# A fused graph-network kernel: messages by a seven-product scheme, sums of h made two blocks ahead, and earlier loads in the front

## The chip, the cores and the metric

The kernel runs on one core of a Trainium2 chip. The metric is device time in microseconds (us) for one execution of the whole program. The profile shows the five engines: PE (TensorE), with its weight loads apart as PEld, DVE (VectorE), ACT (ScalarE), POOL (GpSimd) and SP (SyncE, which here only issues DMAs). ACT also issues DMAs, from its own instruction stream.

## What is computed

Two layers on `x` of shape 128 x 128 x 256 (128 graphs of 128 nodes), all in fp32:

```python
# layer 0, with h = relu(layernorm(x))
s   = h @ w_se.T + b_se                                   # 3 columns
A   = exp(-(sq_i + sq_j - 2 s_i.s_j)) * adj                # sq = sum(s * s)
msg = relu(h @ w_msg.T + b_msg)                            # 256 columns
x_nmp  = A @ msg
x_conv = relu(bn2(conv1d_17(relu(bn1(conv1d_1(h))))) + h)
gi = [x_conv, x_nmp] @ w_ih.T + b_ih;  gh = h @ w_hh.T + b_hh
x  = x + GRU(gi, gh, h)                                    # r, z, n gates
# layer 1: on the first 25 nodes of each graph, five groups of two graph convolutions
```

The rows that the change is about are `msg` and `s`. They are one matrix product, with the 3 columns of `w_se` set beside the 256 of `w_msg`.

## The kernel before

The 128 graphs are worked through in 32 blocks of 4 graphs (`BB`, `NBLK`). h is held transposed: a tile `ht` of 128 partitions (half of the 256 features) x 2 halves x 512 columns (4 graphs x 128 nodes). A bank is one of eight PSUM tiles of 512 fp32 columns, and they are handed out in turn (`bank()`, L92).

**Front.** The 17-wide convolution is done in the frequency domain, for two halves of 64 graphs each. First `weight_spectra` (L158) turns the taps of the convolution into spectra, eight times: taps come in by `taps_load` (L152) into `w2`, four groups of 32 traced matmuls (L165) follow, ACT and DVE copy the banks out (L173, L171), and ACT writes the result to memory (`vd`, L175). Between these groups `heads` (L264) works block by block on the first 64 graphs: `head_load` (L180) brings x in, `head_stats` and `head_norm` do the layer norm on DVE and POOL, `head_turn` transposes it to `ht` (L212) and writes it to memory (`htd`, L214), `head_conv1` (L226) and `head_spectra` (L241) follow. Then `spectral` (L285) multiplies the spectra: for every pair of frequencies it loads a tile `v` from `vd` (L294, three buffers), sums it on POOL (L309), and runs L312 and L317. The second half of the graphs goes through `heads` and `spectral` again. Its first three blocks are begun by `heads_begin` (L251), whose loads are issued from ACT. In the second `spectral`, POOL also makes the weight sums of the gates, a few at a time (`gate_weights`, L331).

In the part of the front up to the end of the first `heads`, the order is written out by hand. So are SP's up to the end of the second `heads`, and POOL's up to the end of the front. Everything else is put in order by a scheduler, which decides each engine's order when the program is built; each engine then works through its own order strictly.

**Gate blocks.** From then on, 32 blocks follow. `gates` (L592) computes three gates by a seven-product scheme: the 256 x 512 product is cut into 2 x 2 quarters, and seven products of quarters, with sums of weights (`sw`) and sums of data (`t`) as operands, take the place of eight. A `unit` (L602) is such a set of seven: each product j has a bank of its own, and is taken out by ACT (`m1`, `m5`: L615, L623), DVE (L617, L620, L627, L630, L633) or POOL (`u4`, L625, which adds two tiles in SBUF; L631). The sums of data come from `gate_inputs` (L578): for xc (the conv branch) and h on POOL, for xn (the message branch) on DVE, four additions each (L586 to L589). They are made in `nxt` (L1021), which runs as a hook at the product j == 4 of the last unit.

After every product, `step` (L1006) lets other work in, alternately one step of `beside_gates` (L954) for the next block and one step of layer 1. `beside_gates(i + 1)` does that block's `messages` (L509), `conv_out` (L490), `edge_terms` (L532), `edges` (L541) and `x_nmp` (L556). In `messages`, each of the 4 graphs has two matmuls of 259 columns with h as the stationary operand (L516), and DVE adds the bias, once for the message (L517) and once for s (L518); ACT does the Relu (L520). The matmuls of `x_nmp` (L563) are 128 columns wide, those of the conv output (L498) too. Between the front and the gate blocks, DVE makes the degrees of layer 1's graphs (`degrees`, L694, with the reduction L698 that waits for a load).

SP's order of loads for a gate block is `load` (L446): ht, adjacency, and the inverse transform's inputs ym and yr.

Of the kernel before, what the change touches and what calls it, by code (L numbers as in the profile page):

```python
# [8 lines left out]
F32 = mybir.dt.float32  # L9
# [4 lines left out]
P = 128  # L14
# [12 lines left out]
HID = 512  # L27

# [46 lines left out]
def gnn_kernel(ctx: ExitStack, tc: tile.TileContext, io, out0: bass.AP, out1: bass.AP):  # L75
# [38 lines left out]
    def constant_loads():  # L114
        nc.sync.dma_start(vec, io["vec"])
        nc.sync.dma_start(wc1, io["wc1"].rearrange("(c p) o -> p c o", p=P))
        nc.sync.dma_start(fd, io["fd"])
# [34 lines left out]
    def taps_load(pool, c, q, queue, split=1):  # L152
        w2 = pool.tile([P, WCH // 4, P], F32, tag="w2", name="w2", bufs=2)
        for t in range(0, WCH // 4, WCH // 4 // split):
            queue.dma_start(w2[:, t:t + WCH // 4 // split], io["w2t"][:, c, q, t:t + WCH // 4 // split])
        return w2
# [94 lines left out]
    def heads_begin(wk, xk, ahead, h):  # L251

        i = h * NBH
        for k in range(ahead):
            head_load(xk, ahead, i + k, nc.scalar)
        yield
        for k in range(3):
            head_stats(wk, i + k)
            yield
            if k < 2:  # L260
                head_norm(i + k)
        head_turn(wk, i)
# [68 lines left out]
    def gate_weights():  # L331
        tt = nc.gpsimd.tensor_tensor
        for k in range(3):
            a11, a12, a21, a22 = gate_blocks(k)
            s2, s3, s4 = (sw[k][:, :, j] for j in range(3))
            tt(s3, a11, a21, op=ALU.subtract)
            tt(a21, a21, a22, op=ALU.add)
            yield
            tt(s2, a21, a11, op=ALU.subtract)
            tt(s4, a12, s2, op=ALU.subtract)  # L340
            yield

    with front as es:
# [7 lines left out]
        with ExitStack() as ws:  # L351
# [8 lines left out]
            taps = [taps_load(wp, *todo[0], nc.sync, split=4)]  # L360
            head_load(xk, ahead, 0, nc.scalar)
            spectra = []

            def some_spectra(k=1):
                for _ in range(k):
                    if not spectra and todo:
                        spectra.append(weight_spectra(wp, *todo.pop(0), taps.pop(0)))
                    if spectra and next(spectra[0], STOP) is STOP:
                        spectra.pop(0)
                        if len(todo) > 1:  # L370
                            taps.append(taps_load(wp, *todo[1], nc.scalar))
                        some_spectra()
# [6 lines left out]
            nc.sync.dma_start(fw, row("fw", 5))  # L379
            head_stats(hk, 0)  # L380
            some_spectra()
            head_norm(0)
            some_spectra()
            head_turn(hk, 0)
            consts = constants()
            next(consts)
            some_spectra()
            head_stats(hk, 1)
# [12 lines left out]
        wms = gw.tile([P, C, D + 3], F32)  # L401
        bms = gw.tile([P, D + 3], F32)
# [4 lines left out]
        def small_loads():  # L407
            nc.sync.dma_start(idm, io["idm"])
            nc.sync.dma_start(wms, io["wms"].rearrange("(c p) o -> p c o", p=P))
            nc.sync.dma_start(bms, row("bms", D + 3))  # L410
# [79 lines left out]
    def conv_out(i):  # L490
# [4 lines left out]
        for o in range(C):  # L495
# [7 lines left out]
            u = wk.tile([P, T], F32, tag="el", name="u", bufs=2)  # L503
            nc.vector.scalar_tensor_tensor(u, ps, sc2[:, o:o + 1], ht[:, o, :], op0=ALU.mult, op1=ALU.add)  # L504
            nc.scalar.activation(xc[:, o, :], u, AF.Relu, bias=sh2[:, o:o + 1])
# [3 lines left out]
    def messages(i):  # L509

        ht = hts[i]
        msg = wk.tile([P, BB, D], F32, tag="msg", name="msg", bufs=1)
        for b in range(BB):
            ps = bank()
            for c in range(C):
                nc.tensor.matmul(ps[:, :D + 3], ht[:, c, b * N:(b + 1) * N], wms[:, c, :], start=c == 0, stop=c == C - 1)  # L516
            nc.vector.tensor_tensor(msg[:, b, :], ps[:, :D], bms[:, :D], op=ALU.add)  # L517
            nc.vector.tensor_tensor(lr[:, 1, b, 0:3], ps[:, D:D + 3], bms[:, D:], op=ALU.add)  # L518
            if b % 2:
                nc.scalar.activation(msg[:, b - 1:b + 1, :], msg[:, b - 1:b + 1, :], AF.Relu)  # L520
                if b == 1:
                    yield
        msgs[i] = msg
        sv = lr[:, 1, :, 0:3]
        nc.vector.tensor_scalar(lr[:, 0, :, 0:3], sv, 2.0, None, op0=ALU.mult)
        s2 = wk.tile([P, BB, 3], F32, tag="sse", name="sse", bufs=2)
        nc.vector.tensor_mul(s2, sv, sv)
        nc.vector.reduce_sum(lr[:, 1, :, 3:4], s2, axis=AX.X)
        nc.vector.tensor_scalar(lr[:, 0, :, 4:5], lr[:, 1, :, 3:4], -1.0, None, op0=ALU.mult)
        yield  # L530
# [25 lines left out]
    def x_nmp(i):  # L556
# [3 lines left out]
        for c in range(C):  # L560
# [4 lines left out]
            if c:  # L565
# [12 lines left out]
    def gate_inputs(i, which=(0, 1, 2)):  # L578

        tt = ts.setdefault(i, {})  # L580
        for k in which:
            d, eng = ((xcs, nc.gpsimd), (xns, nc.vector), (hts, nc.gpsimd))[k]
            d = d[i]
            t = wk.tile([P, 4, H], F32, tag=f"t{k}", name=f"t{k}")
# [401 lines left out]
    degs = degrees(*degree_loads())  # L986
    begin = beside_gates(0)
    while 0 not in A_s:
        next(begin)
    gate_inputs(0, (2, 0))  # L990
# [11 lines left out]
    for i in range(NBLK):  # L1002
# [18 lines left out]
        def nxt():  # L1021
            for _ in first:
                pass
            if i + 1 < NBLK:
                gate_inputs(i + 1)
# [58 lines left out]
def _lay_out(a):  # L1084
# [21 lines left out]
    d["wms"] = cc(np.concatenate([w["w_msg"], w["w_se"]]).T)  # L1106
    d["bms"] = cc(np.concatenate([w["b_msg"], w["b_se"]]))
# [60 lines left out]
```

## Time and profile before

| | |
|---|---|
| runs | 1913.9, 1918.53, 1918.58 us; median 1918.53 |
| the profiled execution's own time | 1919.48 us |
| its span | 1917.7 us |
| mean granted TensorE clock | 0.995 |
| front, up to the first gate block's matmuls | about 490 us |
| one gate block without layer 1 beside it | 36.92 us |
| L516, messages' matmuls | x512, 128x259, 385 ns mean of one |
| L563, x_nmp's matmuls | x512, 128x128, 275 ns mean of one |
| L517 on DVE | x128, 414 ns mean of one |
| L625 on POOL | x128, 728 ns mean of one |

A line such as `L612 PE MATMUL bank<-t,sw 128*128 128x256 f32 x1152 | 291.6, 380` reads: line 612 of the kernel, on TensorE, writes a bank from the tiles t and sw, 1152 instructions with 128 x 256 elements, 291.6 us busy in all, 380 ns each. Matmuls are pipelined, so the duration of one is longer than the distance from one to the next: L516 has 385 ns, while eight of them in a row take 1.75 us. The distance is what counts for TensorE's time. "idle before, releaser" at the end of a line says how long the engine had stood idle and what ended it. The chain of work is followed back from the last instruction; each piece is a start, a duration and what ran. ACTq and SPq are DMA issues from ACT and SP.

### The profile page before, as it was taken

The page shows a single profiled execution, that of the slowest core. Times are in us where ns is not written, and L with a number is a line of the kernel's source. Part 1 is how long each engine was busy: PE and PEld are TensorE (multiplying, and loading weights), DVE is VectorE, ACT ScalarE, POOL GpSimd, SP SyncE. Part 2 cuts the span into 40 slices and gives each one's busy share as a digit, 9 for nine tenths or more (in the row PEclk, how much of TensorE's full clock was granted, in tenths as well). Part 3 has the DMA queues.
Part 4 walks back from the last instruction along what each step waited for, and adds up shares of the span by engine and source line. Part 5 has one row for each costly group of instructions (what it writes and reads, how often), then busy time and mean ns, then how long its engine had stood idle before and what let it go on. Part 6 is the DMA issues. An engine that isn't in the chain of part 4 may idle for free.

```text
span 1917.7 us, 30432 instructions
## 1 busy us (share of the span) xinstructions
PE 1890.3 (99%) x10610; PEld 1646.4 (86%) x10610; DVE 1303.9 (68%) x3247; ACT 720.5 (38%) x1555; POOL 609.1 (32%) x678
## 2 busy tenths in 40 slices
PE   8999999999999999999999999999999999999998
PEld 7888889988788888888888888888888888888887
DVE  5676557744677777777666677777756677787643
ACT  4553114411333343343343443333343434334334
POOL 1012531255234334433322233433322233443300
PEclk9999999999999999999999999999999999999999
DMA  8786896379842333333234433233334434222135
GB/s 322 288 312 226 297 311 235 121 241 306 256 117 73 74 95 76 81 90 106 71 94 97 130 97 87 73 82 108 75 90 97 144 72 107 65 78 71 36 92 151
DMA packets 248872, 265.81 MB, mean 139 GB/s; under 512 B 106866, under 2 KB 223943, under 8 KB 244239
## 3 DMA queue, kind: packets, MB, share of 16 engines
q1 hardware_dynamic: 236639, 196.70, 36.9%
q10 hardware_dynamic: 12080, 67.16, 9.0%
q8 instruction: 85, 1.39, 0.3%
q14 instruction: 68, 0.56, 0.1%
HBM read 178.66 MB, written 85.14 MB: 138 GB/s over the span
## 4 chain that ended last, share of the span: by engine, by line
PE 88%; DMA 4%; DVE 4%; issue 2%; ACT 1%; POOL 1%; SPq 0%; ACTq 0%; POOLq 0%; DVEq 0%
PE bank L612 45%; PE bank L317 6%; PE bank L516 5%; PE bank L937 5%; PE bank L877 5%; PE bank L226 4%; PE bank L312 3%; PE bank L563 3%; PE bank L498 3%; PE bank L241 3%; PE bank L165 2%; PE bank L501 1%; PE bank L788 1%; PE bank L856 1%; DMA v<-vd 1%
## 5 line engine op out<-in xcount | busy, mean ns | idle before, releaser
L612 PE MATMUL bank<-t,sw 128*128 128x256 f32 x1152 | 291.6, 380 | 0.7 <-DVE u L504 0.7
L625 POOL TENSOR_TENSOR u<-u,m 128x256 f32<-128x256 f32 x128 | 93.2, 728 | 612.7 <-ACT m L623 545.0
L612 PEld LDWEIGHTS bank<-t,sw 128*128 128x128 f32 x1152 | 215.8, 191 | 31.1 <-issue 2.3
L612 PE MATMUL bank<-t,wih 128*128 128x256 f32 x768 | 197.2, 379 | 0.0
L612 PEld LDWEIGHTS bank<-t,wih 128*128 128x128 f32 x768 | 143.4, 190 | 19.3 <-issue 0.5
L309 POOL TENSOR_TENSOR vs<-v 128x512 f32<-128x512 f32 x78 | 101.3, 1318 | 114.8 <-DMA v<-vd 49.4
L516 PE MATMUL bank<-wms,ht 128*128 128x259 f32 x512 | 124.1, 385 | 0.0
L226 PE MATMUL bank<-wc,ht 128*128 128x256 f32 x512 | 121.4, 391 | 1.6 <-ACT ht L213 1.6
L612 PE MATMUL bank<-xn,wih 128*128 128x256 f32 x384 | 114.9, 381 | 3.6 <-DVE xn L566 3.6
L612 PE MATMUL bank<-t,whh 128*128 128x256 f32 x384 | 115.0, 381 | 0.0
L612 PE MATMUL bank<-xc,wih 128*128 128x256 f32 x384 | 114.8, 381 | 0.0
L937 PE MATMUL bank<-w,hh 128*125 128x256 f32 (+9 forms) x480 | 113.5, 380 | 1.0 <-DVE hh L882 1.0
L226 PEld LDWEIGHTS bank<-wc,ht 128*128 128x128 f32 x512 | 98.0, 196 | 16.7 <-ACT ht L213 3.5
L516 PEld LDWEIGHTS bank<-wms,ht 128*128 128x128 f32 x512 | 98.3, 192 | 15.1
L612 PE MATMUL bank<-ht,whh 128*128 128x256 f32 x384 | 109.9, 380 | 0.0
L877 PE MATMUL bank<-ax,w 128*128 128x500 f32 (+8 forms) x416 | 107.0, 396 | 0.7 <-DMA w<-in_w_dram 0.7
L520 ACT ACTIVATE msg<-msg 128x512 f32<-128x512 f32 x64 | 40.3, 630 | 174.1 <-DVE msg L517 174.1
L630 DVE TENSOR_TENSOR u<-bank,u 128x256 f32<-128x256 f32 x128 | 53.7, 420 | 73.6 <-PE bank L612 73.5
L196 POOL TENSOR_TENSOR rs<-ve,mhalf 128x4 f32<-128x4 f32 x32 | 32.3, 1009 | 217.8 <-DVE ve L194 217.8
L307 DVE SCALAR_TENSOR_TENSOR s<-X 128x256 f32<-128x256 f32 x78 | 47.3, 612 | 79.4 <-PE bank L317 79.1
L937 PEld LDWEIGHTS bank<-w,hh 128*125 128x125 f32 (+9 forms) x480 | 84.3, 177 | 19.2 <-DVE hh L882 1.4
L657 ACT ACTIVATE nn<-nn,vec 128x512 f32<-128x512 f32 x64 | 46.2, 722 | 133.4 <-DVE nn L656 133.4
(187 smaller groups left out, 4279.5 us busy)
## 6 DMA issues: line engine op xcount, KB each, us to landing
v<-vd SPq DMA_DIRECT2D x80, 512.0 KB
vd<-sp ACTq DMA_DIRECT2D x8, 2560.0 KB
yd<-ys ACTq DMA_DIRECT2D x40, 512.0 KB
w<-in_w_dram SPq DMA_DIRECT2D x40, 512.0 KB
htd<-ht ACTq DMA_DIRECT2D x32, 512.0 KB
ht<-htd SPq DMA_DIRECT2D x32, 512.0 KB
ym<-yd SPq DMA_DIRECT2D x32, 512.0 KB
xt<-in_xT_dram SPq DMA_DIRECT2D x32, 512.0 KB
```

The costliest lines, as they stand in the source:

```text
L226: nc.tensor.matmul(pv[:, bb, :], ht[:, c, b * N:(b + 1) * N], wc1[:, c, :], start=c == 0, stop=c == C - 1)
L241: nc.tensor.matmul(ps[:, bb * 2 * LW:(bb + 1) * 2 * LW], h1[:, 2 * h + bb, c * P:(c + 1) * P], fd, start=True, stop=True)
L309: nc.gpsimd.tensor_tensor(vs, vr, vi, op=ALU.add)
L312: nc.tensor.matmul(p1[:, :D], a[:, c], vs[:, c], start=c == 0, stop=c == C - 1)
L317: nc.tensor.matmul(ps[:, k * D:(k + 1) * D], u[:, c], w[:, c], start=c == 0, stop=c == C - 1)
L498: nc.tensor.matmul(ps[:, b * N:(b + 1) * N], ym[:, b, o * P:(o + 1) * P], idm, start=b == 0, stop=False)
L516: nc.tensor.matmul(ps[:, :D + 3], ht[:, c, b * N:(b + 1) * N], wms[:, c, :], start=c == 0, stop=c == C - 1)
L563: nc.tensor.matmul(ps[:, b * N:(b + 1) * N], msg[:, b, c * P:(c + 1) * P], e[:, b, :], start=True, stop=True)
L612: nc.tensor.matmul(ps, w, d, start=n == 0, stop=n == len(pairs) - 1)
L625: nc.gpsimd.tensor_tensor(got["u4"], got["u2"], got["m5"], op=ALU.add)
L877: nc.tensor.matmul(pv[:, q - q0, :], w1s[k5 + g][:, c, q * P:(q + 1) * P], xv[:, c], start=c == 0, stop=c == C - 1)
L937: nc.tensor.matmul(ps[:n1, :D], hh[:, q, at:at + n1], w2s[k5 + g][:, q, :], start=q == 0, stop=q == HID // P - 1)
```

## The change

- **Messages.** `messages` uses the seven-product scheme as well. The 256 + 3 weight columns get one column of zeros and are cut into two halves of 130 (`MW`); h's quarters and the sums `t` of h are the stationary operands, the weights and three sums of them (`swm`) the moving ones. Each of the seven products has a bank with two matmuls of 130 columns. The bias goes in with product 1 (first half) and with u2 (second half). DVE takes six products out, ACT one (`m5`), POOL adds u4 and the bias to u2. The Relu runs over all of msg at the end, and s is copied from its columns.
- **h's sums.** `gate_inputs(i + 2, (2,))` is called in `nxt` after xc's and xn's for block i + 1; the tile `t2` has two buffers. Before the first block, h's sums for block 0 are made ahead of the messages, and those for block 1 after xc's of block 0.
- **Weights' sums.** `gate_weights` begins with five additions on POOL for the messages' weights and bias.
- **Front.** `vec` is loaded by ACT's queue instead of SP's. The first block of x is loaded by SP after the first quarter of the first taps, instead of by ACT. `w2` has three buffers instead of two, and taps are loaded two spectra ahead instead of one. The first blocks' steps are in another order: the third group of L165 matmuls comes ahead of the first transposes. The loads of `heads_begin` are issued from SP instead of ACT.
- **Small ones.** `conv_out` writes its sum straight to xc, and Relu works in place. In block 0, both halves of xn are copied by ACT.

```diff
-    def taps_load(pool, c, q, queue, split=1):
-        w2 = pool.tile([P, WCH // 4, P], F32, tag="w2", name="w2", bufs=2)
+    def taps_load(pool, c, q, queue, split=1, amid=None):
+        w2 = pool.tile([P, WCH // 4, P], F32, tag="w2", name="w2", bufs=3)
...
         for k in range(ahead):
-            head_load(xk, ahead, i + k, nc.scalar)
+            head_load(xk, ahead, i + k, nc.sync)
...
     def gate_weights():
         tt = nc.gpsimd.tensor_tensor
+        a11, a12, a21, a22 = wms[:, 0, 0], wms[:, 1, 0], wms[:, 0, 1], wms[:, 1, 1]
+        s2, s3, s4 = (swm[:, j] for j in range(3))
+        tt(s3, a11, a21, op=ALU.subtract)
+        tt(a21, a21, a22, op=ALU.add)
+        tt(s2, a21, a11, op=ALU.subtract)
+        tt(s4, a12, s2, op=ALU.subtract)
+        tt(bms[:, 1], bms[:, 1], bms[:, 0], op=ALU.subtract)
+        yield
...
             nc.scalar.dma_start(gt, io["gt"])
-            taps = [taps_load(wp, *todo[0], nc.sync, split=4)]
-            head_load(xk, ahead, 0, nc.scalar)
+            nc.scalar.dma_start(vec, io["vec"])
+            taps = [taps_load(wp, *todo[0], nc.sync, split=4, amid=[lambda: head_load(xk, ahead, 0, nc.sync)])]
...
-                        if len(todo) > 1:
-                            taps.append(taps_load(wp, *todo[1], nc.scalar))
+                        if len(todo) > 2:
+                            taps.append(taps_load(wp, *todo[2], nc.scalar))
...
+            taps.append(taps_load(wp, *todo[2], nc.sync))
             head_stats(hk, 0)
             some_spectra()
             head_norm(0)
-            some_spectra()
-            head_turn(hk, 0)
             consts = constants()
             next(consts)
             some_spectra()
+            some_spectra()
+            head_turn(hk, 0)
...
     def messages(i):
-        ht = hts[i]
-        msg = wk.tile([P, BB, D], F32, tag="msg", name="msg", bufs=1)
-        for b in range(BB):
-            ps = bank()
-            for c in range(C):
-                nc.tensor.matmul(ps[:, :D + 3], ht[:, c, b * N:(b + 1) * N], wms[:, c, :], start=c == 0, stop=c == C - 1)
-            nc.vector.tensor_tensor(msg[:, b, :], ps[:, :D], bms[:, :D], op=ALU.add)
-            nc.vector.tensor_tensor(lr[:, 1, b, 0:3], ps[:, D:D + 3], bms[:, D:], op=ALU.add)
-            if b % 2:
-                nc.scalar.activation(msg[:, b - 1:b + 1, :], msg[:, b - 1:b + 1, :], AF.Relu)
-                if b == 1:
-                    yield
+        msg = wk.tile([P, BB, 2, MW], F32, tag="msg", name="msg", bufs=1)
+        b11, b12, b21, b22 = quarters(hts[i])
+        t1, t2, t3, t4 = (ts[i][2][:, m] for m in range(4))
+        s2, s3, s4 = (swm[:, m] for m in range(3))
+        ops = ((wms[:, 0, 0], b11), (wms[:, 1, 0], b21), (s4, b22), (wms[:, 1, 1], t4), (wms[:, 0, 1], t1), (s2, t2), (s3, t3))
+
+        def product(j):
+            w, d = ops[j - 1]
+            ps = bank()[:, :2 * MW].rearrange("p (b o) -> p b o", b=2)
+            for b in range(2):
+                nc.tensor.matmul(ps[:, b, :], d[:, b * N:(b + 1) * N], w, start=True, stop=True)
+            return ps
...
+        nc.vector.tensor_tensor(m1, product(1), biases(0), op=ALU.add)
+        nc.vector.tensor_tensor(msg[:, 0:2, 0], product(2), m1, op=ALU.add)
+        nc.vector.tensor_tensor(u2, product(6), m1, op=ALU.add)
+        nc.scalar.copy(m5, product(5))
+        nc.gpsimd.tensor_tensor(u4, u2, m5, op=ALU.add)
+        nc.gpsimd.tensor_tensor(u2, u2, biases(1), op=ALU.add)
+        yield
+        nc.vector.tensor_tensor(msg[:, 2:4, 0], product(3), u4, op=ALU.add)
+        nc.vector.tensor_tensor(u3, product(7), u2, op=ALU.add)
+        nc.vector.tensor_tensor(msg[:, 0:2, 1], u3, product(4), op=ALU.subtract)
+        nc.vector.tensor_tensor(msg[:, 2:4, 1], u3, m5, op=ALU.add)
+        mf = msg.rearrange("p b q o -> p b (q o)")
+        for b in range(0, BB, 2):
+            nc.scalar.activation(mf[:, b:b + 2, :D], mf[:, b:b + 2, :D], AF.Relu)
...
-            if c:
+            if c and i:
                 nc.vector.tensor_copy(xn[:, c, :], ps)
...
     degs = degrees(*degree_loads())
+    gate_inputs(0, (2,))
     begin = beside_gates(0)
     while 0 not in A_s:
         next(begin)
-    gate_inputs(0, (2, 0))
+    gate_inputs(0, (0,))
+    gate_inputs(1, (2,))
...
             if i + 1 < NBLK:
-                gate_inputs(i + 1)
+                gate_inputs(i + 1, (0, 1))
+            if i + 2 < NBLK:
+                gate_inputs(i + 2, (2,))
```

## What the change does to the time: the prediction

> **What bounds the kernel now.** I read the busy times first, then the chain of work that ended last, then the chain inside one gate block, then TensorE's and ScalarE's order of time wherever the chain leaves TensorE. Page, parts 1 and 4:
>
> ```profile
> PE 1890.3 (99%) x10610; PEld 1646.4 (86%) x10610; DVE 1303.9 (68%) x3247; ACT 720.5 (38%) x1555; POOL 609.1 (32%) x678
> PE 88%; DMA 4%; DVE 4%; issue 2%; ACT 1%; POOL 1%; SPq 0%; ACTq 0%; POOLq 0%; DVEq 0%
> ```
>
> TensorE sets the end; the other 12% lies in the front (before 565 us) and the tail. The chain in one gate block (start, us, what):
>
> ```profile
> 657.71 1.75 PE bank L516 x8
> 659.46 2.59 PE bank L612 x12
> 662.05 1.75 PE bank L516 x8
> ...
> 679.04 0.89 PE bank L563 x8
> ```
>
> Here nothing but TensorE is on the chain: ten such blocks from 564.17 to 933.36 give 369.19 / 10 = 36.92 us each, with TensorE busy for 369.19 and the granted clock at 1.00. So a matmul saved in a gate block is saved in full, as long as nobody else becomes late. A matmul of the source is two instructions in the trace (L516 has x512 for 32 blocks of 8).
>
> TensorE's and ScalarE's order of time show the front's three places with a long wait and then slow matmuls:
>
> ```profile
> 39.12 1.08 ACT L173 COPY sp<-bank 128x320 f32<-128x320 f32 x3 [2.98 <-issue]
> ...
> 69.94 1.13 PE L165 MATMUL bank<-gt,w 17*128 17x80 f32 x32 [2.42 <-DMA w<-in_w2t_dram]
> 71.00 4.11 PE L241 MATMUL bank<-fd,h 128*128 128x160 f32 x16
> ...
> 149.82 0.38 ACTq L182 DMA_DIRECT2D ln<-in_x_dram  x1
> 154.86 0.35 ACTq L214 DMA_DIRECT2D htd<-ht  x1
> 155.25 0.88 ACT L249 COPY X<-bank 128x160 f32<-128x160 f32 x4 [7.58 <-DMA v<-vd]
> ```
>
> **The change, part by part.** All sums are made against the profiled execution's own 1919.48 us (span 1917.7, 1.8 around it), which lies 0.95 above the median 1918.53.
>
> *Messages, TensorE.* Removed per block: 16 instructions of 259 columns, 2 x 1.75 = 3.50 us (0.2188 each). Added: 7 products x 2 matmuls x 2 = 28 instructions of 130 columns. None has that shape; L563 and L498, 128 columns wide with a new 128-column load each, take 0.89 / 8 = 0.111. Bounds: by columns alone 0.2188 x 130 / 259 = 0.110; if the weight load's mean duration of 191 ns (the PEld row of L563) were the pace, 0.191. L563 has the same loads and is at 0.111, so I take 0.112: 28 x 0.112 = 3.14, a saving of 0.36 us per block, against +1.85 at the other end. The Trainium skill speaks against the change here ("TensorE: Matmul & The Clock Gate", section "LDWEIGHTS (loading the stationary operand)"): a load costs its columns / 1.2 ns, whatever width streams after it. That is 107 ns for each of 28 loads instead of 16, an estimate of 2.99 us of loads against 28 x 0.110 = 3.08 of streaming: level, so the scheme gains but has reached its floor. The row's 0.111 decides. For the 30 blocks inside the dense part: 30 x 0.36 = -10.9.
>
> *Messages, the other engines, per block.* VectorE loses four L517 (0.41) and four L518 (0.07 at their pace), 1.9 us, and gets six additions out of a bank with 260 columns (0.41 each, row L517), one addition between two SBUF tiles (0.42 to 0.93, the L588 row on VectorE without and with GpSimd beside it) and a small copy: 3.0 to 3.6. So +1.1 to +1.7 on 28.4 us busy per block (283.65 / 10): 81 to 82% of the new block. GpSimd gets two additions, 0.73 to 1.17 each (L625, L589); ScalarE one copy of 0.36. All of it lies beside TensorE while banks are free. There are eight banks, and a block now takes seven for messages instead of four. By hand, from 657.6 (first message matmul): products 1, 2, 6, 5 end at 1.8 us, two gate products at 4.4, products 3, 7, 4 at 5.7. VectorE reaches the first addition 4.2 after the start (L517 stood at 661.81, behind L665) and has emptied product 1's bank at 4.6; product 4 asks for it at 5.3. Product 2's bank is empty at 5.6; the next gate product asks at 5.7: no margin. GpSimd is free of the sums at 3.8 (661.3), so u4, ready to start at 6.0, is done at 6.7 to 7.1 and product 3's addition behind it on VectorE waits for nothing. The two Relu now come after the last addition (9.0 to 9.4 instead of 5.6 and 8.0), with the gate's m5 copy, GpSimd's u4 and VectorE's next addition behind them: 1.2 to 2.4 us later than before, on banks that are asked for again at 13. I take nothing for these, and 0.05 us per block (0 to 0.5) for the one without margin: +1.5.
>
> *h's sums two blocks ahead.* The same four GpSimd additions (L586 to L589) per block as before, in the same place of its queue, for block i+2 instead of i+1. No sum is added; a second buffer. Nothing (0 to 0.1 per block either way). The in-place conv output and the five small weight sums on GpSimd (0.4 each, half of L625) hide behind TensorE in the second spectral stage, where GpSimd idles 1.7 us between its L309: nothing.
>
> *Front.* (a) Start: TensorE idles 2.63 us at 7.6 because the first transposes wait for the normalised block. In the built order of the changed kernel a third group of 32 L165 matmuls (1.86 us there) stands before them; its fourth matmul needs a bank that VectorE empties at 8.9. I take -1.5 (0 to -4). (b) At 37.0 ScalarE's issue of a taps load takes 2.00 us, and the copies behind it keep TensorE: 32 L165 from 37.96 to 40.86 (else 1.06), then L226 in 5.07 instead of 3.45. Loss 3.4. In the changed order that issue waits for other, earlier loads. -3.2 (0 to -3.4). (c) At 69.9 taps that were issued at 56.2 land late: wait 2.42, and the next L241 takes 4.06 instead of 2.38. With three buffers each load is issued one spectrum, some 17 us, earlier; it took 13.6. -4.1 (-2 to -4.1). (d) At 142 to 155 the three loads for the second half sit in ScalarE's queue; the third and the next write-back wait for transfers, and the copies behind them come 7.58 late. From 153.4 to 162.3 TensorE does 1.09 + 3.45 us of work: loss 4.35. The loads move to SP, behind 16 loads of v. -4.3 (-1 to -4.4). The skill's rule ("TensorE: Matmul & The Clock Gate", "HAM oscillation") drops TensorE to half clock only after an idle window of about 3.4 us; by it the 2.42 us wait would cost 2.4. The slow L241 row behind it says 4.1, and I go by the row. Sum -13.1; DMA engines are 0.81 to 0.82 busy from 13 to 140 us and get less time for the same bytes, so I give 2 back: -11.
>
> (e) The three loads, 1.5 MB, now fall into the first spectral stage (DMA share 0.87 at 290 GB/s from 200 to 260). On SP they stand ahead of v for p=16; 1.5 MB at 290 GB/s are 5 us, of which v's two tiles of lead (some 10 us, with a landing of 6) hide about 4. +1 (0 to +4). VectorE's statistics of these blocks move with them, behind the same wait: inside that bound.
>
> *Between the stages.* Before, TensorE waits 3.58 us at 505.6 for xn, which stands on VectorE behind a reduction that waits for a 662 KB load until 507.0. Block 0's second xn copy moves to ScalarE. But the messages now need h's sums, which GpSimd cannot start before 489.8: product 6 waits about 1.6, and the lr transposes, behind the longer additions, 2.1; the nh additions and t's sums still stand behind that reduction, and hold banks that products 6 and 7 of block 1 want. I get the first gate sums at 514.2 instead of 513.7: what the moved copy saves, these take back. +0.5 (-3 to +4).
>
> Sum: -10.9 + 1.5 - 11 + 1 + 0.5 = -18.9; 1919.5 - 18.9 = 1900.6 for a profiled execution, 1899.6 at the median's level; I say 1899.5.
>
> **The rivals.** *Only the loop gains* (15%): the front is held by transfers, so a wait removed comes back as a wait for the vd writes (9.3 us each at 139) or for v. For it: DMA share 1.03 from 140 to 160 and 0.98 from 260 to 300. Against it: three of the four waits stand behind an issue in a queue, not behind bandwidth. Then -10.9 + 1.5 + 1.5 = -7.9: 1910.5. *VectorE takes over* (8%): the place is product 2's bank, with its margin of 0.1 us. Each 1 us by which VectorE comes later in each block puts about 0.9 on TensorE; from 0.36 us per block on the loop gains nothing, and from (10.9 + 9.5) / 30 = 0.7 us per block on the whole is slower. At 1.1 us per block: 1918.5 + 33 - 20.4 = 1931. For it: VectorE already at 77% in these blocks and back to back from 653.9 to 666.3. Against it: it idles 1.0, 0.54, 0.87, 0.63 and 1.52 us in the twelve us that follow. *The front gives more* (10%): the early matmuls get to full pace sooner, and the xn wait goes outright: 5 to 8 us more, 1892. *The sums are not what is late at all* is true of the second half of the change: no matmul in the dense part waited for them (0.7 us in 1152), so by itself it moves nothing.
>
> **How the numbers follow.** Forecast 67%, 1899.5, own range 1892 to 1907; the rivals 15, 8 and 10%. The range is 1888 to 1911. A measurement tells about 0.3%, 5.8 us: faster (below 1912.7) takes the forecast, the third rival and most of the first, 0.88; same 0.06; slower 0.06.
>
> **What would show it.** Right: the chain in a gate block still TensorE alone, block period 36.5 to 36.7, the 130-column row at 0.112 per instruction; no L165 wait for taps; the first matmul of the spectral stage near 162 instead of 173; the gate blocks' start 9 to 12 us earlier. Wrong: a wait of message or gate matmuls for VectorE (period above 36.9), a pace of 0.12 or more at 130 columns, a gap in the first spectral stage with v as its releaser, or a start of the gate blocks at 560 or later.

## The result, and the profile after

The changed kernel takes 1906.57 us (median of 6 runs, 1903.92 to 1909.47), beside 1917.7 for the kernel before (6 runs); the ratio is 0.9946 [0.9931, 0.9961]. So it is faster by 0.5%, some 11 us. The forecast of 1899.5 stood against 1918.5, so 19 us less. The time lies inside the range of 1888 to 1911, but of the gain little more than half came. The profiled execution took 1906.46, 13.0 less than the one before.

Parts 1 and 4 of the page of after, and two rows of part 5 (what ran | busy us, mean ns of one | idle time of the engine before it, and what ended most of it). The last row is the one of the weight loads in before:

```profile
PE 1881.7 (99%) x10994; PEld 1646.3 (86%) x10994; DVE 1345.3 (71%) x3246; ACT 723.9 (38%) x1588; POOL 667.7 (35%) x747
PE 92%; DVE 3%; DMA 3%; POOL 1%; issue 1%; ACT 0%; SPq 0%; POOLq 0%; DVEq 0%; ACTq 0%
...
L649 PE MATMUL bank<-xc,wih 128*128 128x256 f32 x384 | 117.0, 386 | 0.7 <-DVE nh L664 0.2
...
L649 PEld LDWEIGHTS bank<-xc,wih 128*128 128x128 f32 x384 | 70.5, 190 | 19.3 <-DVE nh L664 10.8
...
L612 PEld LDWEIGHTS bank<-xc,wih 128*128 128x128 f32 x384 | 72.7, 190 | 10.0
```

TensorE is on 92% of the chain instead of 88, as a shorter front would give. What is new in after is the wait in its last row: over the whole run, the weight loads for the products with xc stood idle 10.8 us behind one addition on DVE (`nh`, L664, in the part of the n gate that comes from h). The row of before has no such wait. The matmul row shows only 0.2 of it, since a load goes ahead of its matmul and the idle time shows there.

The chain of after in one gate block, to be laid beside the one of before, and last the stretch of before that ends its block:

```profile
648.30 1.79 PE bank L535 x16
650.09 2.59 PE bank L649 x12
652.68 1.34 PE bank L535 x12
...
665.51 0.72 PE bank L825 x4
666.23 0.43 PE bank L649 x2
666.66 0.04 issue
666.71 2.86 PE bank L649 x12
...
676.01 3.02 PE bank L612 x14
```

The 28 message instructions take 1.79 + 1.34 = 3.13 us, 0.112 each, instead of 3.50. But the stretch at the end, which in before was one piece of 3.02 us with 14 instructions of L612, is 0.43 + 0.04 + 2.86 = 3.33 here. Of the 0.37 us saved, 0.31 is lost 18 us later in the same block. The order of time shows how, first in before, then in after:

```profile
672.98 0.75 DVE L504 SCALAR_TENSOR_TENSOR u<-bank,bn,ht 128x512 f32<-128x512 f32 x1 [0.63 <-PE bank L501]
...
675.58 0.42 DVE L627 TENSOR_TENSOR nh<-bank,u 128x256 f32<-128x256 f32 x1 [1.52 <-POOL u L625]
676.07 0.40 PEld L612 LDWEIGHTS bank<-xc,wih 128*128 128x128 f32 x2
676.28 0.59 PE L612 MATMUL bank<-xc,wih 128*128 128x256 f32 x2
...
666.23 0.42 DVE L664 TENSOR_TENSOR nh<-bank,u 128x256 f32<-128x256 f32 x1 [1.53 <-PE bank L825]
666.70 0.30 PEld L649 LDWEIGHTS bank<-xc,wih 128*128 128x128 f32 x2 [0.44 <-DVE nh L664]
666.71 0.70 PE L649 MATMUL bank<-xc,wih 128*128 128x256 f32 x2
```

In before DVE has emptied the bank at 676.00, and the load starts at 676.07. In after the addition ends at 666.65 and the load has stood idle for 0.44 us. A load normally starts 0.21 us ahead of its matmul (676.07 and 676.28), which takes up a part of that: TensorE's matmuls show no wait but the 0.04 of issue. The same wait, 0.40 to 0.44 us long, is in 24 of the 29 blocks from the fourth on, and one of 0.57 in another; in the same blocks before has 0.03. (The row names L825 as what ended DVE's wait; in most blocks it names POOL's u4, which here ended at 666.20.)

The front, TensorE's order of time in after:

```profile
65.35 2.44 PE L243 MATMUL bank<-fd,h 128*128 128x160 f32 x16
67.63 3.62 PE L228 MATMUL bank<-wc,ht 128*128 128x256 f32 x16
...
156.77 4.51 PE L243 MATMUL bank<-fd,h 128*128 128x160 f32 x32
161.12 0.60 PE L304 MATMUL bank<-v,X 128*128 128x256 f32 x2
```

And in before, the last of these:

```profile
173.14 0.60 PE L302 MATMUL bank<-v,X 128*128 128x256 f32 x2
```

The wait of 2.42 us for taps is gone, the L243 behind it (L241 before) takes 2.44 instead of 4.11, and the first spectral matmul (L304) starts at 161.12 instead of 173.14.

Where the 13.0 us came from is read from five starting points on TensorE in both traces. "Stage 1" is the first spectral stage up to the second half's first conv matmul; the blocks are counted by the first message matmul of each.

| stretch | before | after | difference | the recorded sum, split the same way |
|---|---|---|---|---|
| start to first spectral matmul | 173.14 | 161.12 | -12.0 | -11 |
| stage 1 | 106.17 | 109.52 | +3.4 | +1 |
| from there to block 0's messages | 210.20 | 208.56 | -1.6 | 0 |
| block 0's to block 3's messages | 94.19 | 95.29 | +1.1 | +0.5 |
| block 3's to block 31's messages (28 blocks) | 1170.34 | 1166.95 | -3.4 | -8.8 |
| from there to the end | 163.66 | 163.26 | -0.4 | -0.6 |

The largest gap by far is in the gate blocks: 0.12 us per block instead of 0.31, as a mean of blocks with and without layer 1. Theory A of the experiments: the messages' Relu hold up a chain through ACT, POOL and DVE that ends at one bank. Theory B: DVE's additional work, or seven banks instead of four, cost it wherever ACT stands.

### The profile page after: what moved, and what is told of

It is laid out like the page before. It is cut to its first block, busy times and chain, and to the rows that moved or that the text cites. A ratio compares the mean times of both kernels' runs of the same rounds, so it can differ in the third digit from the quotient of the medians.

```text
span 1904.7 us, 31441 instructions
## 1 busy us (share of the span) xinstructions
PE 1881.7 (99%) x10994; PEld 1646.3 (86%) x10994; DVE 1345.3 (71%) x3246; ACT 723.9 (38%) x1588; POOL 667.7 (35%) x747
## 4 chain that ended last, share of the span: by engine, by line
PE 92%; DVE 3%; DMA 3%; POOL 1%; issue 1%; ACT 0%; SPq 0%; POOLq 0%; DVEq 0%; ACTq 0%
PE bank L649 45%; PE bank L319 6%; PE bank L974 5%; PE bank L535 5%; PE bank L914 5%; PE bank L228 4%; PE bank L314 3%; PE bank L600 3%; PE bank L243 3%; PE bank L512 3%; PE bank L167 2%; DMA v<-vd 1%; PE bank L515 1%; PE bank L893 1%; PE bank L214 1%; PE bank L825 1%
## 5 line engine op out<-in xcount | busy, mean ns | idle before, releaser
L228 PE MATMUL bank<-wc,ht 128*128 128x256 f32 x512 | 119.9, 387 | 1.4 <-ACT ht L215 1.4
L228 PEld LDWEIGHTS bank<-wc,ht 128*128 128x128 f32 x512 | 97.0, 194 | 15.8 <-ACT ht L215 2.9
L316 ACT COPY k<-bank 128x256 f32<-128x256 f32 x78 | 28.9, 373 | 171.8 <-DVE ys L320 79.7
L649 PEld LDWEIGHTS bank<-xc,wih 128*128 128x128 f32 x384 | 70.5, 190 | 19.3 <-DVE nh L664 10.8
```

Of the source, the lines that this page charges most:

```text
L228: nc.tensor.matmul(pv[:, bb, :], ht[:, c, b * N:(b + 1) * N], wc1[:, c, :], start=c == 0, stop=c == C - 1)
L649: nc.tensor.matmul(ps, w, d, start=n == 0, stop=n == len(pairs) - 1)
```

## The experiments

All ratios are to the kernel before, each from runs of both kernels on one and the same chip; the runs below were made on three chips. Stretches are those of the table above, from the profiled execution.

**The two halves apart.** The kernel before with the front's edits alone, and the changed kernel with the old front:

```diff
 # front_only: before plus these
-        w2 = pool.tile([P, WCH // 4, P], F32, tag="w2", name="w2", bufs=2)
+        w2 = pool.tile([P, WCH // 4, P], F32, tag="w2", name="w2", bufs=3)
...
-            head_load(xk, ahead, i + k, nc.scalar)
+            head_load(xk, ahead, i + k, nc.sync)
...
 # messages_only: after without those
```

> The kernel before with the front's edits alone: vec by ACT, first block by SP, three tap buffers and taps two spectra ahead, order of the first steps, loads of the second half's first blocks by SP. Messages, h's sums and xn's copies as before. Theory from the two traces: the front gains 12.0 up to the first spectral stage, gives 3.4 back in it (a wait for v and slow matmuls behind it) and regains about 1.6 by the first message matmul; nothing of it is lost later: 1917.7 - 10.3 = 1907.4 (1905-1910). The recorded prediction's sum (-11 + 1) says 1907.7. Rival (the wait for the degree load, or the dck wait, which both stand on transfers, take it back): 1911-1916.

> The changed kernel with the old front: messages by seven products, h's sums two blocks ahead, xn's copies by ACT in block 0, but loads, tap buffers and first steps as before. Theory from the two traces: the gate blocks give 0.09-0.11 us each and the step between the stages about nothing, 1917.7 - 2.7 = 1915.0 (1913-1916.5). The recorded prediction's sum (-10.9 + 1.5 + 0.5) says 1908.8. If it comes out near 1909, the loss in the changed kernel is an effect of the new front on the gate blocks, not of the messages.

front_only: 1911.15, ratio 0.9958 [0.9942, 0.9974], so -8.1 us at 1918.5 (-5.0 to -11.1). Its first spectral matmul is at 160.03, stage 1 is 111.28 long. messages_only: 1918.13, ratio 0.999 [0.9974, 1.0006], so -1.9 (-5.0 to +1.2), with 1166.67 for the 28 blocks. Of the first, the value lies nearer to the theory (-10.3) than to the rival (-1.7 to -6.7), but the interval reaches into both. Of the second, the trace's number holds and the recorded -8.9 does not. The two halves add up to -10.0, about what the whole gives, so nothing speaks for a disturbance between them, and the gain that is missing in the gate blocks belongs to the messages.

**h's sums two blocks ahead, alone.**

```diff
-            t = wk.tile([P, 4, H], F32, tag=f"t{k}", name=f"t{k}")
+            t = wk.tile([P, 4, H], F32, tag=f"t{k}", name=f"t{k}", bufs=1 + k // 2)
...
-                gate_inputs(i + 1)
+                gate_inputs(i + 1, (0, 1))
+            if i + 2 < NBLK:
+                gate_inputs(i + 2, (2,))
```

> The kernel before with h's sums made two blocks ahead (second buffer; conv_out in place, which makes the room for it), messages, front and xn's copies as before. Recorded prediction: by itself it moves nothing, since no matmul in the gate blocks waited for a sum: 36.92 per block, time within 2 us of the kernel before. Rival (POOL's additions in the last unit come in another order and hold xc's sums up, or DVE's and POOL's additions meet more often): 0.1-0.3 us per block more, 3 to 9 us slower.

1919.68, ratio 0.9997 [0.9986, 1.0007]; the 28 blocks take 1170.34 us, to the hundredth what they take in before. By itself it moves nothing; it is there so that the messages find their operands.

**The Relu moved, and the Relu doubled.** In the changed kernel the scheduler put both Relu ahead of the gate's m5. An operand made from m5 forces the other order:

```diff
 # relu_later
-        for b in range(0, BB, 2):
-            nc.scalar.activation(mf[:, b:b + 2, :D], mf[:, b:b + 2, :D], AF.Relu)
...
                     got["m5"] = small("m5")
                     nc.scalar.copy(got["m5"], ps)
...
+                    if g == 0:
+                        behind[i] = wk.tile([P, 1], F32, tag="zb", name="zb", bufs=2)
+                        nc.scalar.mul(behind[i], got["m5"][:, :1], 0.0)
...
+            for b in range(0, BB, 2):
+                mf = msgs[i][:, b:b + 2, :D]
+                nc.scalar.activation(mf, mf, AF.Relu, bias=behind.get(i - 1, 0.0))
             inverse = conv_out(i)
 # relu_twice
-            nc.scalar.activation(mf[:, b:b + 2, :D], mf[:, b:b + 2, :D], AF.Relu)
+            for _ in range(2):
+                nc.scalar.activation(mf[:, b:b + 2, :D], mf[:, b:b + 2, :D], AF.Relu)
```

> The changed kernel, with one thing moved: the messages' two Relu on ACT stand behind the gate's m5 copy of product 5 instead of ahead of it (a zero column made from m5, one small ACT instruction per block, is their bias, so that the planner must put them there). Nothing is left out. Theory A (the Relu, which wait for DVE's last addition, hold up m5, then u4 on POOL, DVE's order, and in the end the bank that the first product of the n gate's input part asks for): that wait of about 0.3 us per block goes, the block period falls from 36.84 to 36.55-36.62, and the time from 1906.6 to about 1898 (1895-1900). Theory B (DVE's 1.3 us of additional work per block, or seven banks instead of four, make the loss wherever ACT stands): period stays at 36.8-36.9, time 1905-1908.

> The changed kernel with each of the messages' two Relu run twice in place (the second changes no value): 1.1 to 1.2 us more on ACT ahead of m5 in every block, on an engine that is busy 38% of the time; DVE, POOL and TensorE get no work. Theory A (everything behind the Relu stands on TensorE's path with no slack left): 0.9 to 1.2 us per block more, period 37.7-38.0, time about 1938 (1930-1945). Theory B (DVE's load or the number of banks): ACT has room, period 36.8-37.0, time 1906-1911.

ACT's order of time in the block of after shown above:

```profile
657.76 1.15 ACT L558 ACTIVATE msg<-msg 128x512 f32<-128x512 f32 x2 [7.06 <-DVE msg L554]
658.82 0.35 ACT L660 COPY m<-bank 128x256 f32<-128x256 f32 x1
```

The same place in before:

```profile
665.61 0.63 ACT L520 ACTIVATE msg<-msg 128x512 f32<-128x512 f32 x1 [1.73 <-DVE msg L517]
666.15 0.35 ACT L623 COPY m<-bank 128x256 f32<-128x256 f32 x1
```

And in a block of relu_later, where L1006 is the Relu:

```profile
660.43 0.37 ACT L660 COPY m<-bank 128x256 f32<-128x256 f32 x1 [4.71 <-PE bank L649]
...
662.83 1.34 ACT L1006 ACTIVATE msg<-msg,zb 128x512 f32<-128x512 f32 x2 [1.80 <-DVE msg L554]
```

In after, m5 (L660) starts when the Relu are through, 10.7 us after the block's first message matmul at 648.14. In before it also stood behind a Relu, but came at 8.6 (first message matmul at 657.55), because DVE was done with the messages earlier: its last message addition ended 8.0 us after that matmul, in after 9.9, with DVE at work without a break of more than 0.1 us up to there. So 1.9 of the 2.1 us arise on DVE, where the additional work stands ahead of the Relu. In relu_later m5 starts as soon as TensorE's product is there, 7.3 us after that matmul (653.16). What it is worth on the chain of relu_later:

```profile
653.32 1.79 PE bank L535 x16
655.11 2.59 PE bank L649 x12
657.70 1.34 PE bank L535 x12
...
671.25 3.02 PE bank L649 x14
```

The stretch at the end is 3.02 us in one piece, as in before, and the block period (the time from one block's first message matmul to the next one's, in blocks without layer 1) is 36.55: all of 36.92 - 0.37. In after it is 36.82 to 36.86. The 28 blocks take 1159.83, 10.5 less than in before and 7.1 less than in after. Doubling the Relu gives the other sign. The chain of relu_twice in one block:

```profile
648.83 0.42 DVE z L671
...
661.67 0.43 DVE msg L554
662.13 2.19 ACT msg L559 x4
664.32 0.26 ACT m L661
...
664.65 0.73 POOL u L663
...
665.75 0.74 DVE xc L517
...
671.61 0.44 DVE nh L665
...
672.09 2.86 PE bank L650 x12
```

This is theory A written out: last addition, Relu, m5, u4 on POOL, the additions and the conv output on DVE, and at the end the bank of nh. It also shows what stands ahead of the Relu: from 648.83 to 662.10 almost nothing but DVE's work. The Relu are 2.19 us instead of 1.15, 1.04 more, on an engine that is busy 38% of the time; the period is 37.86 instead of 36.83, 1.03 more, and the time 1934.28, ratio 1.008 [1.0063, 1.0096]: slower than the kernel before. Theory B expected no change in either run and is out as a cause by itself: DVE's work on the messages and the number of banks are the same in all three, and in relu_later nothing of the loss is left. What the two runs show is that the delay reaches TensorE through the Relu ahead of m5. That DVE's additional work is what made these Relu late is read from the traces; no run took that work away and left the Relu where they are.

relu_later itself measured 1905.45, ratio 0.9928 [0.9911, 0.9944], only some 3 us below the changed kernel instead of 7. Its profiled execution reached block 0's messages at 483.4 instead of 479.2, though the front's edits are the same. A second pair of runs, on one chip, bears on this.

> The changed kernel, unaltered, on the same chip as the next three, so that they can be compared with it directly. Expected as before: ratio to the kernel before 0.9946 (0.993 to 0.996). The question is the front: executions with the same front have shown the first message matmul at 479.2, 480.9 and 483.4 us, so a difference of a few us between two runs may be the front's alone.

> The same kernel as relu_later, beside the changed kernel on one chip. Its block period was 36.55 against 36.84, 7.1 us over the 28 blocks from the fourth on, but its time was only some 3.5 us better by the ratios; its front was 4.2 us late in the profiled execution. If that is the front's scatter, its median is now 5 to 9 us below the changed kernel's; if moving the Relu costs something elsewhere, 1 to 4.

after_again: 1907.61, 0.9942 [0.993, 0.9955]. relu_later_again: 1904.38, 0.9919 [0.9906, 0.9931], with 1159.82 for the 28 blocks again, and block 0's messages at 482.4 again (after_again: 479.0). The medians differ by 3.2 us, the ratios by 0.0023 or 4.4 us, where 5 to 9 were expected for mere scatter. Each ratio has an interval of some 2.4 us either way, so neither reading is excluded. In the blocks, 7 us are there both times; ahead of them, 4.2 and 3.4 are given back in the profiled executions. In relu_later, 2.5 of this lie before the first spectral matmul: ACT's issue of a taps load near 36 us took 1.98 us instead of 0.91, and the L228 behind it 5.41 instead of 3.72. In relu_later_again, 2.4 lie in stage 1 (111.97 against 109.55), where TensorE's mean granted clock was 0.97 instead of 1.00. Both vary between executions of the same kernel or the same front. With the Relu moved as well, relu_and_spread (below) reached block 0's messages at 479.2, so a late front does not go with the moved Relu; eight executions with that front, or with three loads in another place, gave 479.0 to 483.4. How much the medians owe to this is open.

**The wait for dck.** In after's block 1, TensorE waits for DVE, which waits for small loads of layer 1. TensorE's order of time in after:

```profile
549.78 1.22 PE L649 MATMUL bank<-t,whh 128*128 128x256 f32 x2 [2.83 <-DVE u L667]
```

The stretches around it (start and end, length, busy time of PE, PEld, DVE, ACT, POOL, granted clock, DMA share, GB/s):

```profile
546.50:549.80 3.30, 0.47 (x4) 0.07 (x2) 0.92 (x3) 0.06 (x1) 0.00 (x0) 0.91 0.76 195
549.80:552.50 2.70, 2.70 (x11) 1.67 (x11) 2.41 (x7) 1.49 (x3) 1.28 (x2) 0.50 0.31 80
552.50:555.50 3.00, 3.00 (x8) 2.59 (x9) 1.48 (x5) 2.78 (x7) 0.88 (x2) 0.50 0.54 174
```

In before the same place shows two waits of 0.67 and 0.70. One run tried to move DVE's part of it to where the loads have long landed:

```diff
+            nc.vector.tensor_scalar(one, outs[max(outs)][:, 0, :1], 0.0, 1.0, op0=ALU.mult, op1=ALU.add)
...
-            nc.vector.tensor_add(nt[:n, :n], nt[:n, :n], ident[:n, :n])
+            nc.vector.scalar_tensor_tensor(nt[:n, :n], ident[:n, :n], one[:n], nt[:n, :n], op0=ALU.mult, op1=ALU.add)
```

> relu_later with one more thing moved: layer 1's first five additions and products of the adjacency (nt, dck) on DVE get an operand that exists only from gate block 10 on, so that DVE no longer waits for the dck loads in the second gate block. No value changes. Theory: in the changed kernel TensorE loses 2.8 us there for DVE's u, and about 3 more in the matmuls that follow at a lower granted clock; the distance from the third to the fourth block's messages, 43.4 to 44.5, falls to about 38-39, and the time 4 to 6 us below relu_later. Rival: the same loads are then waited for in blocks 11 and 12 (period there longer by as much): no gain.

1904.14, ratio 0.9922 [0.9909, 0.9936]. The distance from the third to the fourth block's messages fell from 43.45 (relu_later_again) to 36.55, and the one from the thirteenth to the fourteenth grew from 53.63 to 60.96: -6.9 and +7.3. The rival was right. There are three buffers for dck: in held_back SP issued three of these loads at 529.24, and the next one at 907.21, after DVE had used the first at 906.90. So the wait goes where DVE goes. TensorE's order of time of held_back, in the later place:

```profile
915.42 0.70 PE L649 MATMUL bank<-t,sw 128*128 128x256 f32 x2 [1.70 <-DVE xc L517]
...
919.97 0.76 PE L583 MATMUL bank<-lt 5*128 5x128 f32 x2 [0.92 <-DVE hn L823]
```

A run with more buffers for dck would settle whether the wait can be removed; none was made.

**The front's parts.**

```diff
 # taps_three: before plus
+            taps.append(taps_load(wp, *todo[2], nc.sync))
...
-                        if len(todo) > 1:
-                            taps.append(taps_load(wp, *todo[1], nc.scalar))
+                        if len(todo) > 2:
+                            taps.append(taps_load(wp, *todo[2], nc.scalar))
 # (and three buffers for w2)
 # loads_on_act: after, but
-            head_load(xk, ahead, i + k, nc.sync)
+            head_load(xk, ahead, i + k, nc.scalar)
 # loads_spread: after, but
             head_load(xk, ahead, i + k, nc.sync)
-        yield
+            yield
...
-        amid = {p: lambda: next(begin, None) for p in range(16, NP_, 4) if p != 20}
+        amid = {p: lambda: next(begin, None) for p in range(8, NP_, 4) if p != 20}
```

> The kernel before with the tap buffers alone: three instead of two, and taps loaded two spectra ahead. The recorded prediction takes -4.1 for this (the wait of 2.42 us at 69.9 and the 1.7 us by which the matmuls behind it are slow), and it moves the other waits of the front but little: first spectral matmul at 169 instead of 173.1, time 1913-1916. Rival (the transfers of the front take it back, or the wait on ACT's end loads grows by as much): first spectral matmul at 172-173, no gain.

1914.18, ratio 0.9974 [0.9962, 0.9986]: -5.0 us (-2.7 to -7.3), where -4.1 was on record. Its profiled execution was quicker than that: first spectral matmul at 165.70, -7.4. By the L226 that starts at 74.95 in before it has gained 6.4, of which 1.4 is an L226 at 40 us that takes 3.72 instead of 5.13.

> The changed kernel with one line back: the three loads of the second half's first blocks issued from ACT's queue again, as before. In the changed kernel they are issued from SP at 188.1 us ahead of v, and the first spectral stage is 109.2 to 112.0 us long instead of 106.2. Theory (the two terms of the recorded sum belong together): the first spectral matmul comes 4 to 5 us later (165-166 instead of 161), the stage falls back to about 106, and the net is within 2 us of the changed kernel: 1905-1909. Rival (the loss in the stage comes from elsewhere, such as v standing behind a larger backlog): the stage stays at 109 or more and the time is 4 to 5 us above the changed kernel, 1911.

1912.4, ratio 0.9963 [0.9951, 0.9975], between the two expectations: about 3.5 us slower than the changed kernel (0.9942 and 0.9946), with intervals that just overlap. The first spectral matmul is at 166.67. ACT's queue shows the old picture again, ahead of TensorE's waits:

```profile
137.16 1.38 ACTq L184 DMA_DIRECT2D ln<-in_x_dram  x1
143.97 0.38 ACTq L184 DMA_DIRECT2D ln<-in_x_dram  x1
148.66 0.35 ACTq L216 DMA_DIRECT2D htd<-ht  x1
149.05 0.89 ACT L251 COPY X<-bank 128x160 f32<-128x160 f32 x4 [6.78 <-DMA v<-vd]
...
149.59 1.35 PE L243 MATMUL bank<-fd,h 128*128 128x160 f32 x8 [1.52 <-ACT X L251]
```

So the wait behind ACT's queue is real: of the 5.6 us against after's 161.12, 3.4 arose behind the L228 at 67.63 and 69.81, the rest at a short wait and an L228 of 5.41 near 40. But stage 1 was 109.96 long here too, with a wait of 2.87 us six frequencies later than the one of 2.56 in after; the one in after ended with a sum of v on POOL, for this one the profile names nothing that ended it.

> The changed kernel with the same three loads issued from SP one at a time, at p = 8, 12 and 16 of the first spectral stage, instead of all three at p = 16. Theory (1.5 MB in one piece ahead of v outrun v's lead; 0.5 MB does not): the wait for v at p = 16 and the slow matmuls behind it go, the stage is 106 to 107.5 us long, the time 2 to 5 us below the changed kernel: 1902-1905. Rival (the stage is held by the amount of data, not by its burst): 109-112 and 1906-1908.

1909.46, ratio 0.9943 [0.9924, 0.9961], stage 1 108.38: the rival, no gain. The stage was 105.8, 106.2, 106.3 and 109.2 long in the kernels with the old front or the taps alone (taps_three, before, messages_only, two_ahead), 109.5 to 112.0 in seven executions with the loads from SP at p = 16, 108.4 and 110.4 with them spread, 110.0 with them on ACT. That the burst is the cause is not shown.

**The best version.** relu_later and loads_spread together:

> relu_later and loads_spread together, as the best version that the runs point to. If both act by their own: block period 36.55, first spectral stage 106-107.5 us, ratio to the kernel before about 0.990 (1899-1902). If the spread gives nothing, 0.992 (1904) as relu_later.

1900.07, ratio 0.9895 [0.9874, 0.9917]: faster than both kernels. The block period is 36.55, stage 1 110.37. What it has over relu_later alone (0.9919 and 0.9928) does not come from a shorter stage, and the intervals overlap. The Relu's place is shown: by the block period, and by the three ratios of 0.9895 to 0.9928 below 0.9942 and 0.9946. The spread is not.

## Why the prediction was right, and where it was 7 us off

- **What bounds the kernel.** Right: a matmul saved in a gate block is saved in full "as long as nobody else becomes late". Someone does.
- **Messages on TensorE.** Right. 0.112 per instruction of 130 columns was taken from rows of 128, and 3.13 us were measured. The 0.37 us arrive in full wherever layer 1 fills the block: two of the longer blocks fell from 67.26 to 66.88 and from 57.73 to 57.36.
- **The other engines: the step that failed.** The prediction saw the chain and its delay ("The two Relu now come after the last addition", "1.2 to 2.4 us later than before"; m5 is 2.1 later) and then wrote "on banks that are asked for again at 13. I take nothing for these". The bank that matters is asked for at 18.4 us, further along the same chain. In before, DVE emptied it only 0.07 us before the weight load that asks for it (rows above), and had itself waited 0.63 for TensorE on the way: the chain followed TensorE, and would have come earlier with it. In after, the delay has used up that wait, and the chain hangs on the Relu: DVE's addition starts 18.09 us after the block's first message matmul, 18.03 in before, while TensorE gets there 0.37 earlier. So the load is held up for some 0.4, and the matmuls behind it for 0.31 in the block shown: 0.21 because the first one starts later, 0.10 because it now starts with its load instead of behind it. The term is 0.25 us per block over the 28 blocks, the 0.375 of relu_later less 0.12 (0.27 to 0.31 in a block without layer 1, nothing in the two kinds of longer blocks named above). The prediction put it at nothing, and its 0.05 on product 2's bank, where TensorE waited for nothing. DVE's own additional work was sized rightly: 1345.3 - 1303.9 = 41.4 us in 32 blocks, 1.3 each (1.1 to 1.7 on record). That it stands ahead of the Relu, and so on this chain, was not followed.
- **h's sums two blocks ahead.** Right: nothing (1170.34 us with and without).
- **Front.** -12.0 in the profiled execution against -11, and -8.1 for the whole front by front_only against -10 with stage 1. TensorE's rows of the two executions split the -12.0: the start (a) gave 0.75 where 1.5 were on record, ACT's issue (b) 2.45 for 3.2, the taps (c) 4.1 for 4.1 (5.0 measured alone), the end loads (d) 4.5 for 4.3 (3.4 by loads_on_act). The parts were 13.1 on record, less 2 for a DMA backlog; what failed to come lies in (a) and (b). (b) was luck: ACT's issue took 2.00 us in before and 0.91 in after, but in the ten executions with the new taps and first steps it took 0.7 to 0.9 six times and 2.0 to 2.3 four times (2.25 in loads_on_act), with the same loads ahead of it. Stage 1 was mis-sized: +3.4 against +1, inside its 0 to +4. The wait for v was foreseen (2.56 us in after); the lower clock behind it was not, and whether the three loads cause the wait is open.
- **Between the stages.** +1.1 against +0.5. The xn wait of 3.58 us went, as expected, and waits of 1.39 for h's sums and 2.23 for lr came, as expected (1.6 and 2.1). The dck wait, which costs more in after, was in no step.
- **The rivals.** "Only the loop gains" was wrong from both ends: the front gained and the loop hardly. "VectorE takes over" had the right mechanism, a bank that is emptied too late. It is VectorE that empties it, and VectorE's work that begins the delay, but at another place, by way of ScalarE and GpSimd, and at a price below its own break-even point of 0.36 per block. Of "The front gives more", the wait for xn did go outright, but other waits took its place.
- **What would show it.** Of the signs of being right, the pace of 0.112, no wait for taps, the first spectral matmul at 161.1 and gate blocks that start 10.3 us earlier came; the block period of 36.5 to 36.7 did not, and at 36.82 to 36.86 it stayed just below the sign of being wrong, 36.9. One sign of being wrong came, the gap in stage 1 with v behind it. So the number was reached with a front that gave what was expected, in part by luck, and with four tenths of the gain in the gate blocks (-3.4 of -8.8).

## What to carry over

When work is taken off the bounding engine, follow the longest chain through the other engines to its last bank and compare its margin there with the time saved: a chain that has been delayed until it no longer follows the bounding engine needs a margin of that size. Read the margin at the weight load, which asks for the bank ahead of its matmul (0.07 us here, where the matmul's row suggests 0.28). Work that nobody needs soon, such as a Relu on a result that is used some 10 us later, belongs behind the copies that free banks (m5 here); what a scheduler orders has to be looked up in the built order, and forced by a data dependence where needed. A wait on loads with few buffers moves with its consumer and is not removed by postponing it (-6.9 and +7.3 us here).

## What the runs showed of the hardware

After some short idle times TensorE's granted clock fell for several us. The 2.83 us of idle in after's block 1 were followed by 0.50 for 5.7 us (rows above); in stage 1, 2.56 us by a clock of 0.62 over the next 4.5:

```profile
204.49 2.08 PE L314 MATMUL bank<-vs,X 128*128 128x256 f32 x4 [2.56 <-POOL vs L311]
...
202.00:204.50 2.50, 0.01 (x1) 0.01 (x1) 2.50 (x7) 0.75 (x2) 1.33 (x2) 1.00 1.09 383
204.50:209.00 4.50, 4.50 (x13) 3.75 (x14) 1.24 (x3) 0.37 (x1) 3.79 (x3) 0.62 1.12 376
```

So these two waits cost TensorE 1.7 to 2 times their own length (2.56 + 4.5 x 0.38 = 4.3; 2.83 + 5.7 x 0.50 = 5.7). It does not follow every such wait. The one at the same place in after_again, the same kernel, was longer, and the clock stayed at 1.00:

```profile
206.43 1.13 PE L314 MATMUL bank<-vs,X 128*128 128x256 f32 x4 [2.67 <-POOL vs L311]
...
206.40:210.90 4.50, 4.47 (x21) 3.96 (x22) 0.92 (x1) 0.74 (x2) 3.88 (x3) 1.00 1.07 389
```

Among waits of 2.2 to 3.2 us the fourteen traces have both cases, so the length of a wait does not tell which will be followed by a low clock.

Second, stage 1, which is filled by DMA (share 0.81 to 0.86), took 105.8 to 112.0 us in fourteen executions. In these, TensorE's waits of over 0.1 us add up to 0.9 to 5.9 us, and the lower clock takes 0, 1.7 or 3.4 us (the share by which its mean lies below 1.00, times the length of the stage); what is left is 103.9 to 105.2. The gate blocks without layer 1 agree to 0.04 us within an execution: differences of a few us between kernels have to be read by stage.
